# Two gather tiles instead of three, a reordered last step, and interleaved rows in a spiking recommender kernel on one Trainium2 core

## The chip, the cores and the metric

The kernel runs on one core of a Trainium2 chip. A core has five engines that run their own instruction streams and meet through semaphores: TensorE (PE; its weight loads are shown apart as PEld), VectorE (DVE), ScalarE (ACT), GpSimd (POOL) and SyncE (SP), and 16 DMA engines that all of them share. The metric is the device time of one execution in microseconds (us); the median of three runs stands for the kernel.

## The reference

1024 users have 50 items each, out of a table of 100001 rows of 128 numbers. Row 0 of the table counts as zero. All arithmetic is float32.

```python
emb = emb_table.at[0].set(0.0)
e = emb[seq]                              # (1024, 50, 128)
prefix = jnp.cumsum(e, axis=1)
t_idx = jnp.arange(1, T + 1)
denom = jnp.minimum(t_idx[None, :], lengths[:, None])
uF = prefix / denom[:, :, None]
mean = uF.mean(axis=0); var = uF.var(axis=0)      # over the users, for each step and column
y = (uF - mean) * lax.rsqrt(var + BN_EPS) * gamma + beta
# for each of the 50 steps, with x the step's y and v starting at 0:
#   v = v + (x - v) / 2;  spike = v >= 1;  v = v - spike
uF_out = spikes.mean(axis=0)              # (1024, 128)
scores = uF_out @ emb.T                   # (1024, 100001)
```

The output is 1024 x 100001 float32, 409.6 MB, and writing it is most of the traffic.

## The kernel before

The work is written in program order under a manual schedule: each engine runs its instructions in the order in which the code emits them, and a tile pool of `bufs=n` makes the writer of a tile wait until the tile n places earlier has been read.

**Opening (lines 174 to 252).** SP loads the indices (`idx`, line 175, users n*128 + p on partition p, column block n), the lengths, row 0 of the table, gamma and beta, and then 38 blocks of 1024 table rows that the second stage needs (`fetch`). `isz` and `rb` are two tiles of 1024 columns that are transposed on TensorE: one marks the indices that are 0, the other holds 1/length. They take two of the three tiles of the pool `gather`.

**The 50 steps (lines 296 to 370).** The users lie on the free axis, the 128 columns of the table on the partitions. For step t:

- `gather(t + 2)` at the head of the step issues eight indirect DMAs on GpSimd (line 195), each of which fetches 128 table rows of 512 B into a column block of the tile `e`. Step t reads its own tile `e`, gathered two steps ahead. Only the first of the eight waits for the tile to be free.
- TensorE adds the transposed rows to the running sums in the two PSUM banks `pre[0]` and `pre[1]` (line 308, eight transposes); `correct` (line 268) adds in advance a term that takes row 0 of the table out again. `correct(t + 1)` overwrites nothing, but it must follow Vector's reading of `pre` in step t, so the transposes of step t + 1 come after the last uF of step t.
- Vector makes uF, half by half (`uF`, line 317; `bs`, line 318), and from it mean and variance (`mv`, line 322). ScalarE takes the root (line 326) and subtracts the mean (line 327).
- Vector completes the scale `a` (lines 333 to 338). Meanwhile it finishes the previous step: `rest` (line 284) makes `negv` = spike - v from `d`, which ScalarE made as v - 1 (`over`, line 280), and `spiked` (line 287) adds the spikes to `count`.
- ScalarE applies scale and shift (line 342), Vector adds -0.5 * negv (`step`, line 345): the new v.

In steps 42 and 44 two blocks of the table are transposed and split ahead of time (`prepare`: TensorE, ScalarE and Vector).

In the last step, `rest` and `spiked` of step 48 come first, ahead of the first uF. Behind the loop the last v is made in three groups of columns, 128, 512 and 384, each with its own tile of counts (`countA`, `countB`, `countC`): ScalarE computes x for all three, Vector does `step` and `spiked` for A, then both for B and C. TensorE warms up on 16 dummy transposes (line 377) meanwhile. A block of 128 users is then one 128-column piece of these counts, n = 0 to 7, the first being `countA`.

**The scores (lines 395 to 491).** For chunks of 2, 3 or 6 blocks of 1024 table rows, and for each of the eight blocks of users, TensorE multiplies the counts with a high and a low part of the table block (line 153), Vector and ScalarE take turns in scaling the result out of PSUM (lines 469 and 471), and SP stores up to 24 KB for each of 128 output rows (`store`, line 162): rows n*128 to n*128 + 127. ScalarE issues the loads of the remaining table blocks. New blocks are transposed and split between the products.

Of the kernel before, what the change touches and what calls it, by code (L numbers as in the profile page):

```python
# [12 lines left out]
F32 = mybir.dt.float32  # L13
# [4 lines left out]
AF = mybir.ActivationFunctionType  # L18
ALU = mybir.AluOpType

P = 128
BN_EPS = 1e-5
# [3 lines left out]
BANK = 512  # L26
# [10 lines left out]
def rec_kernel(  # L37
# [9 lines left out]
    nc = tc.nc  # L47
    B, T = seq.shape
    N, D = table.shape
    NB = B // P  # L50
    assert D == P and B == HALF and T <= P // 2


# [9 lines left out]
    countA = const.tile([P, P], F32R, tag="countA", name="countA")  # L63
    countB = const.tile([P, BANK], F32R, tag="countB", name="countB")
    countC = const.tile([P, B - BANK - P], F32R, tag="countC", name="countC")
# [93 lines left out]
            )  # L159

    def store(n, c0, o):
        nc.sync.dma_start(out=out[n * P : (n + 1) * P, c0 : c0 + o.shape[1]], in_=o)


    with ExitStack() as ph:
        once = ph.enter_context(tc.tile_pool(name="once", bufs=1))
        lp = ph.enter_context(tc.tile_pool(name="lif", bufs=1))
        sp = ph.enter_context(tc.tile_pool(name="stats", bufs=3))
        up = ph.enter_context(tc.tile_pool(name="uF", bufs=2))
        gp = ph.enter_context(tc.tile_pool(name="gather", bufs=3))  # L170
        accp = ph.enter_context(tc.tile_pool(name="acc", bufs=1, space=bass.MemoryType.PSUM))
        vp = ph.enter_context(tc.tile_pool(name="v", bufs=1, space=bass.MemoryType.PSUM))

        idx = once.tile([P, NB, T], I32, tag="idx", name="idx")
        nc.sync.dma_start(out=idx, in_=seq.rearrange("(n p) t -> p n t", p=P))
        len_i = once.tile([P, NB], I32, tag="len_i", name="len_i")
        nc.sync.dma_start(out=len_i, in_=lengths.rearrange("(n p) -> p n", p=P))
        r0 = once.tile([P, D], F32, tag="r0", name="r0")
        nc.sync.dma_start(out=r0, in_=table[0:1, :].to_broadcast([P, D]))
        gb = once.tile([P, 2], F32, tag="gb", name="gb")  # L180
        nc.sync.dma_start(out=gb[:, 0:1], in_=gamma.rearrange("(d o) -> d o", o=1))
        nc.sync.dma_start(out=gb[:, 1:2], in_=beta.rearrange("(d o) -> d o", o=1))
        first = group(0)
# [8 lines left out]
        def gather(t):  # L192
            es[t] = gp.tile([P, B], F32, tag="e", name=f"e_{t}")
            for n in range(NB):
                nc.gpsimd.indirect_dma_start(  # L195
                    out=es[t][:, n * P : (n + 1) * P],
                    out_offset=None,
                    in_=table,
                    in_offset=bass.IndirectOffsetOnAxis(ap=idx[:, n, t : t + 1].bitcast(U32), axis=0),
                )  # L200

        make_identity(nc, ident)
        isz = gp.tile([P, NB, P], F32, tag="e", name="isz")
        rb = gp.tile([P, NB, P], F32, tag="e", name="rb")
        gather(0)

        nc.vector.memset(isz, 0.0)
# [2 lines left out]
        zps = vp.tile([P, B], F32, tag="v1", name="zps")  # L210
        for n in range(NB):
            nc.tensor.transpose(zps[:, n * P : (n + 1) * P], isz[:, n, :], ident)
        zT = once.tile([P, B], F32R, tag="zT", name="zT")
        nc.scalar.copy(zT, zps)
        r0hi = once.tile([P, D], F32R, tag="r0hi", name="r0hi")
        nc.scalar.copy(r0hi, r0)
        r0n = once.tile([P, D], F32, tag="r0n", name="r0n")
# [14 lines left out]
        rlen = once.tile([P, B], F32, tag="rlen", name="rlen")  # L232
        nc.vector.tensor_copy(rlen, rps)

        hgb = once.tile([P, 2], F32, tag="hgb", name="hgb")
        nc.vector.tensor_scalar_mul(hgb[:, 0:1], gb[:, 0:1], 0.25)
        nc.vector.tensor_scalar_mul(hgb[:, 1:2], gb[:, 1:2], 0.5)
        eps = once.tile([P, 1], F32, tag="eps", name="eps")
        nc.vector.memset(eps, BN_EPS)
# [2 lines left out]
        count = once.tile([P, B], BF16, tag="count", name="count")  # L242
        nc.vector.memset(count, 0.0)

        negv = once.tile([P, B], F32, tag="negv", name="negv")
# [3 lines left out]
        pre = [accp.tile([P, BANK], F32, tag=f"pre{h}", name=f"pre{h}") for h in range(B // BANK)]  # L249
# [33 lines left out]
        def rest(d, v):  # L283
            nc.vector.scalar_tensor_tensor(negv, d, 0.0, v, ALU.is_ge, ALU.subtract)  # L284

        def spiked(out, cs, v):
            nc.vector.scalar_tensor_tensor(out, v, V_TH, count[:, cs], ALU.is_ge, ALU.add)  # L287

        whole = slice(0, B)
        halves = [slice(h * BANK, (h + 1) * BANK) for h in range(B // BANK)]  # L290
        v = None
# [3 lines left out]
        gather(1)  # L295
        for t in range(T):
            last = t == T - 1
            if t + 2 < T:
                gather(t + 2)
            e = es.pop(t)  # L300
            if last:
                rest(d, v)
                spiked(count, whole, v)
            uF = up.tile([P, B], F32, tag="uF", name=f"uF_{t}")
            bs = sp.tile([P, B // BANK, 6], F32, tag="bs", name=f"bs_{t}")
            for h, cs in enumerate(halves):
                for k in range(0, BANK, P):
                    nc.tensor.matmul(  # L308
                        pre[h][:, k : k + P],
                        lhsT=e[:, h * BANK + k : h * BANK + k + P],  # L310
                        rhs=ident,
                        start=False,
                        stop=last,
                        is_transpose=True,
                        skip_group_check=True,
                    )
                nc.vector.scalar_tensor_tensor(uF[:, cs], rlen[:, cs], 1.0 / (t + 1), pre[h], ALU.max, ALU.mult)  # L317
                nc.vector.bn_stats(bs[:, h, :], uF[:, cs])  # L318
            if not last:
                correct(t + 1, l)  # L320
            mv = sp.tile([P, 2], F32, tag="mv", name=f"mv_{t}")
            nc.vector.bn_aggr(mv, bs.rearrange("p h s -> p (h s)"))  # L322


            r = sp.tile([P, 1], F32, tag="r", name=f"r_{t}")
            nc.scalar.activation(r, mv[:, 1:2], AF.Sqrt, bias=eps)  # L326
            nc.scalar.activation(uF, uF, AF.Identity, bias=mv[:, 0:1], scale=-1.0)


            if t and not last:  # L330
                rest(d, v)

            nc.vector.reciprocal(r, r)
            q = sp.tile([P, 1], F32, tag="q", name=f"q_{t}")
            nc.vector.scalar_tensor_tensor(q, mv[:, 1:2], BN_EPS, r, ALU.add, ALU.mult)
            nc.vector.tensor_scalar(q, q, r, 3.0, ALU.mult, ALU.subtract)
            a = sp.tile([P, 1], F32, tag="a", name=f"a_{t}")
            nc.vector.tensor_scalar(a, q, r, hgb[:, 0:1], ALU.mult, ALU.mult)  # L338


            def x(vt, cs):
                nc.scalar.activation(vt, uF[:, cs], AF.Identity, bias=hgb[:, 1:2], scale=a)  # L342

            def step(vt, cs):
                nc.vector.scalar_tensor_tensor(vt, negv[:, cs], -0.5, vt, ALU.mult, ALU.add)  # L345

            if not last:
                vt = vp.tile([P, B], F32, tag=f"v{t % 2}", name=f"v_{t}")
                x(vt, whole)
                if t:  # L350
                    spiked(count, whole, v)
                step(vt, whole)
                v = vt
                d = over(t, v)
                if t + 2 < T:
                    l = only(t + 2)

                if t in (T - 8, T - 6):
                    q = (t - T + 8) // 2
                    pair(q)  # L360
                    prepare(q, vp.tile([P, HALF], F32, tag="v1", name=f"pt_{q}"))
                    if q == TWICE - 1:
                        for k in range(TWICE):
                            rows[GROUP + k] = first[:, k, :]
                        nc.sync.dma_start(
                            out=first[:, :TWICE, :],
                            in_=table[GROUP * HALF : (GROUP + TWICE) * HALF, :].rearrange(
                                "(q p k) d -> p q (k d)", p=P, k=KQ
                            ),
                        )  # L370
# [5 lines left out]
        for k in range(2 * KQ):  # L376
            nc.tensor.transpose(warm[:, k % KQ * P : (k % KQ + 1) * P], ident, ident)
        vC = vp.tile([P, B - BANK - P], F32, tag="v1", name="vC")
        groups = [
            (slice(0, P), pre[0][:, :P], countA),  # L380
            (slice(P, P + BANK), pre[1], countB),
            (slice(P + BANK, B), vC, countC),
        ]
        for cs, vt, _ in groups:
            x(vt, cs)
        cs, vt, first = groups[0]
        step(vt, cs)
        spiked(first, cs, vt)
        for cs, vt, _ in groups[1:]:
            step(vt, cs)  # L390
        for cs, vt, c in groups[1:]:
            spiked(c, cs, vt)


# [2 lines left out]
        for q, (pool, tag, po) in enumerate(((gp, "e", po0), (up, "uF", po1))):  # L397
            o = pool.tile([P, HALF], F32, tag=tag, name=f"o_0_{q}")
# [26 lines left out]
    for c, W in enumerate(WIDTHS):  # L425
# [30 lines left out]
        for n in range(NB):  # L456
            if c == 0 and n == 0:
                continue
            pool, tag, most = turns[blocks % len(turns)]
            blocks += 1  # L460
            o = pool.tile([P, most * HALF], F32, tag=tag, name=f"o_{c}_{n}")
# [16 lines left out]
            if c or n > 1:  # L478
                store(n, q0 * HALF, o[:, : min(N, q1 * HALF) - q0 * HALF])
# [3 lines left out]
            if n in (1, 4) and c >= MIDDLE and to_fetch < parts:  # L483
                g, k = divmod(to_fetch - TWICE, GROUP)
                if k or to_split >= (g - 1) * GROUP + TWICE:
                    if k == 0:
                        r = group(g)
# [23 lines left out]
```

## Time and profile before

| | us |
|---|---|
| median of three runs | 1648.53 (1646.59 to 1648.60) |
| the profiled execution: its time | 1649.66 |
| the profiled execution: its span | 1647.8 |
| first gather issued | 3.96 |
| last gather issued | 565.6 |
| first store issued | 586.71 |
| busy: PE, DVE, ACT, POOL | 1069.7, 944.0, 669.2, 381.4 |

The span is cut in two stages by the first store. Ahead of it DMA engines move some 47 GB/s once the opening loads are done (about 60 us), and the granted TensorE clock is 0.50; behind it they move 416 GB/s. A line of the timeline gives start, duration, engine, source line, operation and tiles, and in brackets how long the engine sat idle before it and what ended that. "issue" is idle time for which the profile shows no cause, "remote" is an end that it puts down to no engine or queue of this core. In the table of stretches each row gives, for a piece of the span, busy time and number of instructions of PE, PEld, DVE, ACT and POOL, the granted clock, the DMA engines' busy share and what they moved. In the list of waits the figures are the total, the number and the longest. The starts of matmuls are recorded, their ends are modelled.

### The profile page before, as it was taken

What the parts mean: (1) busy time and instruction counts of PE and PEld (TensorE: products, weight loads), DVE (VectorE), ACT (ScalarE), POOL (GpSimd) and SP (SyncE); (2) the same over time, 40 slices, a digit from 0 to 9 for tenths busy, and PEclk for the clock granted to TensorE, in tenths of its full rate; (3) what the DMA queues carried; (4) which work ended last, traced back from release to release, by engine and by line L of the source; (5) the groups of instructions that cost most, each with busy time, mean ns of one, the idle gap of its engine ahead of it and who ended that gap; (6) DMA issues with size and microseconds to landing.
All of it is one profiled execution on the core that took longest, in us unless ns stands there. A gap on an engine that the chain in (4) does not pass through costs nothing.

```text
span 1647.8 us, 12231 instructions
## 1 busy us (share of the span) xinstructions
PE 1069.7 (65%) x4450; PEld 816.8 (50%) x4450; DVE 944.0 (57%) x1122; ACT 669.2 (41%) x697; POOL 381.4 (23%) x406
## 2 busy tenths in 40 slices
PE   4233332222322488888988888888887888888884
PEld 2022221111211376666866666666666666666763
DVE  5366665656665866556755455555555555555552
ACT  2133332323322455455644444444444444444442
POOL 7676666666666500000000000000000000000000
PEclk7555555555555589999999999989999999999998
DMA  9511111111111269999999999999999999999998
GB/s 345 209 50 46 46 47 46 45 46 49 46 45 46 64 285 416 405 421 418 399 425 429 430 429 423 416 434 418 427 427 416 416 421 417 428 427 423 396 431 342
DMA packets 53689, 488.12 MB, mean 296 GB/s; under 512 B 11995, under 2 KB 12796, under 8 KB 32380
## 3 DMA queue, kind: packets, MB, share of 16 engines
q1 hardware_dynamic: 32256, 429.81, 62.0%
q0 software_dynamic: 12800, 26.24, 5.9%
q10 hardware_dynamic: 8572, 31.28, 4.8%
q8 instruction: 35, 0.57, 0.1%
q14 instruction: 26, 0.21, 0.0%
HBM read 77.69 MB, written 409.60 MB: 296 GB/s over the span
## 4 chain that ended last, share of the span: by engine, by line
DMA 45%; DVE 20%; PE 11%; another core or an unknown queue 10%; ACT 7%; issue 4%; POOL 1%; ACTq 0%; SPq 0%; DVEq 0%
DMA scores<-o 45%; PE po L153 10%; ACT o L471 5%; DVE bs L318 4%; DVE uF L317 3%; DVE v L345 3%; DVE negv L284 3%; DVE count L287 2%; ACT v L342 2%; DVE o L469 1%; POOL e L195 1%; PE pre L268 1%; DVE a L338 1%; DVE mv L322 1%
## 5 line engine op out<-in xcount | busy, mean ns | idle before, releaser
L469 DVE TENSOR_SCALAR o<-po 128x1024 f32<-128x1024 f32 x391 | 464.4, 1221 | 344.7 <-DMA scores<-o 310.4
L471 ACT ACTIVATE o<-po 128x1024 f32<-128x1024 f32 (+1 forms) x391 | 389.7, 1018 | 538.8 <-DMA scores<-o 324.6
L195 POOL DMA_INDIRECT e<-in_L_rec_emb_table,idx x400 | 380.7, 952 | 184.6 <-issue 114.9
L153 PE MATMUL po<-pairs,countB 128*128 128x512 f32 x1136 | 305.1, 414 | 59.8 <-ACT o L471 42.8
L268 PE MATMUL pre<-zT,ls 128*128 128x512 f32 x100 | 78.7, 789 | 364.1 <-DVE uF L317 267.1
L153 PEld LDWEIGHTS po<-pairs,countB 128*128 128x128 f32 x1136 | 218.0, 197 | 122.9 <-ACT o L471 57.9
L153 PE MATMUL po<-pairs,countC 128*128 128x512 f32 x852 | 236.4, 424 | 44.8 <-ACT o L471 44.8
L268 PEld LDWEIGHTS pre<-zT,ls 128*128 128x128 f32 x100 | 28.8, 289 | 407.7 <-DVE uF L317 297.2
L153 PEld LDWEIGHTS po<-pairs,countC 128*128 128x128 f32 x852 | 167.0, 203 | 90.7 <-ACT o L471 56.3
L317 DVE SCALAR_TENSOR_TENSOR uF<-rlen,pre 128x512 f32<-128x512 f32 x100 | 68.0, 680 | 168.1 <-remote 101.2
L146 DVE TENSOR_TENSOR pairs<-pt,pairs 128x1024 fp32r<-128x1024 f32 x71 | 86.3, 1222 | 93.3 <-ACT pairs L145 93.2
L326 ACT ACTIVATE r<-mv,eps 128x1 f32<-128x1 f32 x50 | 14.7, 295 | 283.2 <-DVE mv L322 179.5
L123 PE MATMUL pt<-ident,rows 128*128 128x128 f32 x782 | 113.8, 294 | 8.7 <-issue 4.9
L123 PEld LDWEIGHTS pt<-ident,rows 128*128 128x128 f32 x782 | 103.5, 155 | 27.5 <-issue 13.2
L308 PE MATMUL pre<-ident,e 128*128 128x128 f32 x400 | 101.0, 422 | 16.1 <-DMA e<-in_L_rec_emb_table,idx 14.9
L153 PE MATMUL po<-hi,countB 128*128 128x512 f32 x216 | 89.1, 412 | 19.4 <-ACT o L471 16.8
L308 PEld LDWEIGHTS pre<-ident,e 128*128 128x128 f32 x400 | 83.6, 221 | 31.6 <-DMA e<-in_L_rec_emb_table,idx 21.8
L153 PE MATMUL po<-lo,countB 128*128 128x512 f32 x216 | 86.7, 403 | 0.0
L280 ACT ACTIVATE d<-v,less 128x1024 bf16<-128x1024 f32 x49 | 54.5, 1113 | 63.6 <-DVE v L345 45.4
L153 PE MATMUL po<-hi,countC 128*128 128x512 f32 (+1 forms) x162 | 68.4, 422 | 15.7 <-ACT o L471 15.7
L145 ACT CAST pairs<-pt 128x1024 fp32r<-128x1024 f32 x71 | 71.8, 1012 | 15.4 <-PE pt L123 15.2
L153 PE MATMUL po<-pairs,countA 128*128 128x512 f32 x284 | 71.3, 394 | 8.2 <-ACT o L471 8.1
(67 smaller groups left out, 844.5 us busy)
## 6 DMA issues: line engine op xcount, KB each, us to landing
scores<-o SPq DMA_DIRECT2D x96, 3072.0 KB
scores<-o SPq DMA_DIRECT2D x32, 1536.0 KB
scores<-o SPq DMA_DIRECT2D x30, 1024.0 KB
rows<-in_L_rec_emb_table ACTq DMA_DIRECT2D x19, 1536.0 KB
scores<-o SPq DMA_DIRECT2D x8, 2896.5 KB
rows<-in_L_rec_emb_table SPq DMA_DIRECT2D x6, 3072.0 KB
e<-in_L_rec_emb_table,idx POOLq DMA_INDIRECT x400
rows<-in_L_rec_emb_table SPq DMA_DIRECT2D x1, 1024.0 KB
```

The costliest lines, as they stand in the source:

```text
L123: nc.tensor.transpose(pt[:, k0 : k0 + kw], r[:kw, k0 : k0 + D], ident[:kw, :kw])
L145: nc.scalar.copy(vh, vp)
L146: nc.vector.tensor_tensor(vl, vp, vh.bitcast(F32), ALU.subtract)
L153: nc.tensor.matmul(po[:, :kw], lhsT=counts[n], rhs=part[:, k0 : k0 + kw], start=j == 0, stop=j == 1,)
L195: nc.gpsimd.indirect_dma_start(out=es[t][:, n * P : (n + 1) * P], out_offset=None, in_=table, in_offset=bass.IndirectOffsetOnAxis(ap=idx[: ...
L268: nc.tensor.matmul(pre[h], lhsT=l, rhs=zT[:, h * BANK : (h + 1) * BANK], start=t == 0, stop=False, skip_group_check=True,)
L280: nc.scalar.activation(d, v, AF.Identity, bias=less)
L308: nc.tensor.matmul(pre[h][:, k : k + P], lhsT=e[:, h * BANK + k : h * BANK + k + P], rhs=ident, start=False, stop=last, is_transpose=True, ...
L317: nc.vector.scalar_tensor_tensor(uF[:, cs], rlen[:, cs], 1.0 / (t + 1), pre[h], ALU.max, ALU.mult)
L318: nc.vector.bn_stats(bs[:, h, :], uF[:, cs])
L469: nc.vector.tensor_scalar_mul(o[:, h0 : h0 + hw], po[:, :hw], 1.0 / T)
L471: nc.scalar.mul(o[:, h0 : h0 + hw], po[:, :hw], 1.0 / T)
```

## The change

The change has four parts.

1. The pool `gather` has two tiles instead of three. `isz` and `rb` take the two tiles of the pool `uF` instead. `gather(t + 2)` is issued behind the transposes of step t, whose tile it overwrites, instead of at the head of the step.
2. In the last step the comparison and the addition to `count` for step 48 are two GpSimd instructions of 1024 columns (`s`, in the room of `zT`), and `rest` stands between the two halves of uF. The order on Vector is: uF and bs of the first half, `rest`, `near`, uF and bs of the second half.
3. The first 128 columns of the last step run on Vector alone: `near` = -0.5 * negv + beta/2, `centred` = (uF - mean) * (-gamma/4), `q` in another grouping of the same factors, `vA` = centred * q + near, then `countA`. `a` is computed behind that for the other two groups. ScalarE subtracts the mean for groups B and C behind the loop. On Vector, `step` and `spiked` follow each other within a group.
4. Partition p holds users 8p to 8p + 7 instead of p, 128 + p, ...: the loads of indices and lengths are contiguous for each partition, and a store of block n writes the output rows 8p + n.

```diff
--- before.py
+++ after.py
@@ -48,6 +48,7 @@
     B, T = seq.shape
     N, D = table.shape
     NB = B // P
+    outs = out.rearrange("(p n) c -> n p c", n=NB)
     assert D == P and B == HALF and T <= P // 2
 
 
@@ -159,7 +160,7 @@
             )
 
     def store(n, c0, o):
-        nc.sync.dma_start(out=out[n * P : (n + 1) * P, c0 : c0 + o.shape[1]], in_=o)
+        nc.sync.dma_start(out=outs[n, :, c0 : c0 + o.shape[1]], in_=o)
 
 
     with ExitStack() as ph:
@@ -167,14 +168,14 @@
         lp = ph.enter_context(tc.tile_pool(name="lif", bufs=1))
         sp = ph.enter_context(tc.tile_pool(name="stats", bufs=3))
         up = ph.enter_context(tc.tile_pool(name="uF", bufs=2))
-        gp = ph.enter_context(tc.tile_pool(name="gather", bufs=3))
+        gp = ph.enter_context(tc.tile_pool(name="gather", bufs=2))
         accp = ph.enter_context(tc.tile_pool(name="acc", bufs=1, space=bass.MemoryType.PSUM))
         vp = ph.enter_context(tc.tile_pool(name="v", bufs=1, space=bass.MemoryType.PSUM))
 
         idx = once.tile([P, NB, T], I32, tag="idx", name="idx")
-        nc.sync.dma_start(out=idx, in_=seq.rearrange("(n p) t -> p n t", p=P))
+        nc.sync.dma_start(out=idx, in_=seq.rearrange("(p n) t -> p n t", n=NB))
         len_i = once.tile([P, NB], I32, tag="len_i", name="len_i")
-        nc.sync.dma_start(out=len_i, in_=lengths.rearrange("(n p) -> p n", p=P))
+        nc.sync.dma_start(out=len_i, in_=lengths.rearrange("(p n) -> p n", n=NB))
         r0 = once.tile([P, D], F32, tag="r0", name="r0")
         nc.sync.dma_start(out=r0, in_=table[0:1, :].to_broadcast([P, D]))
         gb = once.tile([P, 2], F32, tag="gb", name="gb")
@@ -200,8 +201,8 @@
                 )
 
         make_identity(nc, ident)
-        isz = gp.tile([P, NB, P], F32, tag="e", name="isz")
-        rb = gp.tile([P, NB, P], F32, tag="e", name="rb")
+        isz = up.tile([P, NB, P], F32, tag="uF", name="isz")
+        rb = up.tile([P, NB, P], F32, tag="uF", name="rb")
         gather(0)
 
         nc.vector.memset(isz, 0.0)
@@ -232,8 +233,9 @@
         rlen = once.tile([P, B], F32, tag="rlen", name="rlen")
         nc.vector.tensor_copy(rlen, rps)
 
-        hgb = once.tile([P, 2], F32, tag="hgb", name="hgb")
+        hgb = once.tile([P, 3], F32, tag="hgb", name="hgb")
         nc.vector.tensor_scalar_mul(hgb[:, 0:1], gb[:, 0:1], 0.25)
+        nc.vector.tensor_scalar_mul(hgb[:, 2:3], gb[:, 0:1], -0.25)
         nc.vector.tensor_scalar_mul(hgb[:, 1:2], gb[:, 1:2], 0.5)
         eps = once.tile([P, 1], F32, tag="eps", name="eps")
         nc.vector.memset(eps, BN_EPS)
@@ -295,12 +297,11 @@
         gather(1)
         for t in range(T):
             last = t == T - 1
-            if t + 2 < T:
-                gather(t + 2)
             e = es.pop(t)
             if last:
-                rest(d, v)
-                spiked(count, whole, v)
+                s = once.tile([P, B], F32, tag="zT", name="s")
+                nc.gpsimd.tensor_single_scalar(s, d, 0.0, ALU.is_ge)
+                nc.gpsimd.tensor_tensor(count, count, s, ALU.add)
             uF = up.tile([P, B], F32, tag="uF", name=f"uF_{t}")
             bs = sp.tile([P, B // BANK, 6], F32, tag="bs", name=f"bs_{t}")
             for h, cs in enumerate(halves):
@@ -316,6 +317,12 @@
                     )
                 nc.vector.scalar_tensor_tensor(uF[:, cs], rlen[:, cs], 1.0 / (t + 1), pre[h], ALU.max, ALU.mult)
                 nc.vector.bn_stats(bs[:, h, :], uF[:, cs])
+                if last and h == 0:
+                    rest(d, v)
+                    near = once.tile([P, P], F32, tag="r0", name="near")
+                    nc.vector.tensor_scalar(near, negv[:, :P], -0.5, hgb[:, 1:2], ALU.mult, ALU.add)
+            if t + 2 < T:
+                gather(t + 2)
             if not last:
                 correct(t + 1, l)
             mv = sp.tile([P, 2], F32, tag="mv", name=f"mv_{t}")
@@ -324,7 +331,13 @@
 
             r = sp.tile([P, 1], F32, tag="r", name=f"r_{t}")
             nc.scalar.activation(r, mv[:, 1:2], AF.Sqrt, bias=eps)
-            nc.scalar.activation(uF, uF, AF.Identity, bias=mv[:, 0:1], scale=-1.0)
+            if last:
+                centred = once.tile([P, P], F32, tag="r0hi", name="centred")
+                nc.vector.tensor_scalar(centred, uF[:, :P], mv[:, 0:1], hgb[:, 2:3], ALU.subtract, ALU.mult)
+                w = sp.tile([P, 1], F32, tag="w", name="w")
+                nc.vector.tensor_scalar_add(w, mv[:, 1:2], BN_EPS)
+            else:
+                nc.scalar.activation(uF, uF, AF.Identity, bias=mv[:, 0:1], scale=-1.0)
 
 
             if t and not last:
@@ -332,10 +345,18 @@
 
             nc.vector.reciprocal(r, r)
             q = sp.tile([P, 1], F32, tag="q", name=f"q_{t}")
-            nc.vector.scalar_tensor_tensor(q, mv[:, 1:2], BN_EPS, r, ALU.add, ALU.mult)
-            nc.vector.tensor_scalar(q, q, r, 3.0, ALU.mult, ALU.subtract)
             a = sp.tile([P, 1], F32, tag="a", name=f"a_{t}")
-            nc.vector.tensor_scalar(a, q, r, hgb[:, 0:1], ALU.mult, ALU.mult)
+            if last:
+                nc.vector.tensor_scalar(q, w, r, r, ALU.mult, ALU.mult)
+                nc.vector.scalar_tensor_tensor(q, q, 3.0, r, ALU.subtract, ALU.mult)
+                vA = once.tile([P, P], F32, tag="r0n", name="vA")
+                nc.vector.scalar_tensor_tensor(vA, centred, q, near, ALU.mult, ALU.add)
+                spiked(countA, slice(0, P), vA)
+                nc.vector.tensor_mul(a, q, hgb[:, 0:1])
+            else:
+                nc.vector.scalar_tensor_tensor(q, mv[:, 1:2], BN_EPS, r, ALU.add, ALU.mult)
+                nc.vector.tensor_scalar(q, q, r, 3.0, ALU.mult, ALU.subtract)
+                nc.vector.tensor_scalar(a, q, r, hgb[:, 0:1], ALU.mult, ALU.mult)
 
 
             def x(vt, cs):
@@ -376,19 +397,12 @@
         for k in range(2 * KQ):
             nc.tensor.transpose(warm[:, k % KQ * P : (k % KQ + 1) * P], ident, ident)
         vC = vp.tile([P, B - BANK - P], F32, tag="v1", name="vC")
-        groups = [
-            (slice(0, P), pre[0][:, :P], countA),
-            (slice(P, P + BANK), pre[1], countB),
-            (slice(P + BANK, B), vC, countC),
-        ]
+        groups = [(slice(P, P + BANK), pre[1], countB), (slice(P + BANK, B), vC, countC)]
         for cs, vt, _ in groups:
+            nc.scalar.activation(uF[:, cs], uF[:, cs], AF.Identity, bias=mv[:, 0:1], scale=-1.0)
             x(vt, cs)
-        cs, vt, first = groups[0]
-        step(vt, cs)
-        spiked(first, cs, vt)
-        for cs, vt, _ in groups[1:]:
+        for cs, vt, c in groups:
             step(vt, cs)
-        for cs, vt, c in groups[1:]:
             spiked(c, cs, vt)
```

## The prediction

> **What bounds the kernel now.** I read the page's slices first: the span is two stages. In the first 14 slices GpSimd is busy and the DMA engines lie at a tenth or two; from slice 15 on the DMA engines are full.
>
> ```profile
> POOL 7676666666666500000000000000000000000000
> PEclk7555555555555589999999999989999999999998
> DMA  9511111111111269999999999999999999999998
> ```
>
> The stage of stores (first store at 586.7, end 1647.8, 1061.1 us) moves 416 GB/s with a DMA share of 0.99; no engine there is the bound, so it takes what its bytes take. The change reaches the time by when that stage begins and by how the stores are laid out. So I went to the 50 steps, first to GpSimd's waits and then to busy time by stretches cut where GpSimd starts again after a wait (columns: PE, PEld, DVE, ACT, POOL busy and count, clock, DMA share, GB/s).
>
> ```profile
> POOL e L195 <- issue: 114.9, 377, 0.3
> POOL e L195 <- remote: 55.5, 10, 7.8
> ```
>
> ```profile
> 264.00:309.10 45.10, 13.18 (x40) 8.82 (x40) 28.88 (x50) 14.62 (x16) 30.38 (x32) 0.50 0.18 47
> ...
> 354.30:398.80 44.50, 13.18 (x40) 8.83 (x40) 28.68 (x50) 14.62 (x16) 30.45 (x33) 0.50 0.19 48
> 398.80:433.50 34.70, 9.39 (x30) 6.62 (x30) 21.28 (x37) 10.96 (x12) 22.81 (x24) 0.50 0.18 46
> ```
>
> 400 gathers at 0.94 us busy and 0.30 of issue are 1.25 each, 500 us; ten long waits add 55. In the steady stretches the pattern repeats every 32 gathers (four steps): 40 us of issuing, 5.3 of waiting, 45.1. What GpSimd waits for shows in the timeline of one such stretch.
>
> ```profile
> 288.49 1.91 PE L308 MATMUL pre<-ident,e 128*128 128x128 f32 x8
> ...
> 303.95 0.69 DVE L317 SCALAR_TENSOR_TENSOR uF<-rlen,pre 128x512 f32<-128x512 f32 x1 [9.68 <-issue]
> ...
> 308.89 0.69 DVE L317 SCALAR_TENSOR_TENSOR uF<-rlen,pre 128x512 f32<-128x512 f32 x1 [3.53 <-remote]
> ...
> 309.13 0.94 POOL L195 DMA_INDIRECT e<-in_L_rec_emb_table,idx  x1 [5.30 <-remote]
> ```
>
> The transposes of step 24 are recorded within 2 us at 288.5, yet the two L317 that wait for them run at 303.95 and 308.89. TensorE's semaphore steps in the trace come at 290.6, 293.4, 296.2, 298.3, 301.1, 306.7: one per 2 to 3 us instead of per 0.2. So TensorE really crawls there, while GpSimd issues on until it needs the tile of step 24 (last issue 302.88, its data moved by 305.1). TensorE is quick again only some 4 us after the gather traffic has stopped. I don't know the cause. I read it as something that fills with gather traffic and drains at a fixed rate: after each stop some 24 us pass until TensorE slows, and cycles of 32 and of 24 gathers give nearly one rate (45.1/32 = 1.41, 34.7/24 = 1.446 us a gather). Vector's own chain needs only 7.35 us a step (v at 321.20 and 328.55), GpSimd 10.0.
>
> The last bound is the tail, from v of step 48 to the first product:
>
> ```profile
> 576.98 1.22 DVE L284 SCALAR_TENSOR_TENSOR negv<-d,v 128x1024 f32<-128x1024 bf16 x1 [1.18 <-ACT d L280]
> 578.12 1.22 DVE L287 SCALAR_TENSOR_TENSOR count<-v,count 128x1024 bf16<-128x1024 f32 x1
> 579.25 0.68 DVE L317 SCALAR_TENSOR_TENSOR uF<-rlen,pre 128x512 f32<-128x512 f32 x1
> ...
> 583.22 0.27 DVE L338 TENSOR_SCALAR a<-q,r,hgb 128x1 f32<-128x1 f32 x1
> 584.11 0.29 DVE L345 SCALAR_TENSOR_TENSOR pre<-negv,pre 128x128 f32<-128x128 f32 x1 [0.61 <-ACT pre L342]
> 584.44 0.29 DVE L287 SCALAR_TENSOR_TENSOR countA<-pre,count 128x128 fp32r<-128x128 f32 x1
> ```
>
> Here Vector is the path: 1.18 of waiting for d, then negv and count, before the last uF, whose transposes had ended at 572.9.
>
> **What the Trainium skill says.** *GPSIMD Engine Reference*, § Elementwise — side-by-side cycle accounting: an fp32 add of two tensors of 2048 columns takes 4497 ns on GpSimd; the trace before has no arithmetic there to compare. *SBUF — State Buffer*, § SBUF: two separate sides: GpSimd and a Vector operation in a two-port mode, or with two SBUF inputs, exclude each other for a whole instruction; not visible before, since GpSimd only gathers (a gather took 1.16 and 2.26 us once each, the rest 0.94). *DMA: Bandwidth & Descriptors*, § Latency and other measured facts: HBM rows whose pitch is a large power of two copy at half rate or less, and a few KiB of padding restore it. § Specifications of the same page: pieces under 512 B are below line rate; the idx load here is of 200 B pieces, 1024 of them, and took 2.94 us.
>
> **The change part by part.**
> *Start.* idx becomes 128 runs of 1600 B. GpSimd's first gather waits for it (starts at 3.96). A load of that size still has its fixed latency: a gather lands 2.3 us after its start, so I take 2.2 us instead of 2.94, -0.7; bounds -1.2 and 0. isz and rb move to the uF pool: gathers of step 1 lose a wait that cost nothing (they follow at 1.25), and uF of steps 0 and 1 wait for transposes that were over at 6.5 and 12. Nothing.
>
> *Two tiles.* A gather of step t+2 now waits for the transposes of step t, not t-1, and all later gathers queue behind it on GpSimd; nothing else is in that queue until the last step, SP's isn't passed. In clear running the wait is free: gathers of step t take 10.0 us, land 2.3 after, transposes take 1.9, so tile t is free 4 to 5 us after its last issue, while GpSimd is busy 10 us with t+1. In a slow patch I count from a restart R. With two tiles only one landed tile is waiting, the steps run just behind the gathers, and the transposes of R's third tile end at R+21.4. TensorE slows at R+24; GpSimd still issues the fourth and fifth tile until R+40, then stops, as it does now (302.88 + 0.94 is R+39.8 from 264.0). So a cycle stays 32 gathers in 45 us: 0. The cover is 24 - 21.4 = 2.6 us; the rival below prices its loss. A gain is left at the end: now the steps lag the gathers (last gather lands at 567.9, transposes end at 572.9, v of step 48 ends at 575.8, made later by the two `prepare` calls); just behind them, transposes would end near 568.5 and v near 567.3, up to 8.5 us sooner. Where the last slow patch falls decides how much of that comes; it can also fall on the last tile, about +5. I take -3.
>
> *Last step.* uF of the first half starts at v's end, 575.8. In order: uF and bs 1.4, negv 1.22 (d was ready at 576.9), near some 0.25 (128 columns; r0n, the same shape, took 0.23), second half 1.4: aggregate at 580.0 instead of 582.0. After the reciprocal: two q of 0.2, then vA and countA at 0.33 each, without a, the two ACT calls and their 0.61 of waiting: the first product at 582.0 instead of 584.85, -2.85. centred and w lie under ACT's square root (0.36 of idle now). countB and countC: centring moves behind on ACT (0.65 and 0.5), but TensorE has eight products (2.6 us) of countA before it needs countB, which comes 2.3 after countA: hidden; without cover 0.5. GpSimd's count: compare and add of 1024 columns, by the page's figure an estimated 1 + 2.3 us from 577.0, ready near 580.4, needed at 581.6; hidden if so, and at double price 2 us late. Near and centred may have to wait for GpSimd's add by the exclusion above, up to 2 us. So -2.85 to 0; I take -1.5.
>
> *Stores.* Row pitch within a store goes from 400,004 B to 3,200,032 B: 3 MiB and 53 KiB, far from an aliasing multiple by the page's figures. Packets, bytes and order stay. I take 0; bounds -5 and +20 (2% of 1061).
>
> Sum: -0.7 - 3 - 1.5 = -5.2 on the profiled execution: span 1647.8 to 1642.6, its time 1649.66 (1.86 around the span) to 1644.5. The median of the runs, 1648.53, lies 1.1 below that execution, so 1643.3, given as 1643.5.
>
> **The rivals.** *Two tiles lose gathers (slower).* Place: the wait of the first gather of tile t+2. If TensorE slows before the third tile's transposes are through, that is before R+21.4, GpSimd stops at R+30 and each cycle is 24 gathers. The trace prices it: 1.446 against 1.41 us, 0.037 x 360 gathers = +13 us, less 2.2 for start and tail: 1659.5. For it: the onset varies from 21 to 32 us. Against: one steady drain rate, which would cancel most of it. *Nothing but the ends.* Cycles and lag stay, the port lock eats part of the tail: -1 to -3, 1646.5. *The stores' layout costs 1%*: +10.6 - 5.2, 1654. All 416 GB/s are near what this stage ever shows (up to 442 in 2 us), so it could hardly gain.
>
> **How the numbers follow.** Forecast 0.45 (1636 to 1646), two tiles losing 0.27 (1652 to 1668), ends only 0.20 (1644.5 to 1648), stores 0.08. A measurement of this kernel tells about 0.2%, 3.3 us, from no change. Faster (under 1645.2): most of the forecast and a little of the ends, 0.42; same: the rest of both, 0.24; slower: 0.34. The range 1636 to 1662 leaves out one in ten on each side; the forecast's own is 1636 to 1646.
>
> **What would show it.** Right: gather stretches still at 1.40 to 1.42 us a gather, ten long waits of GpSimd near 5 us, last L317 of step 49 nearer to the last gather than 13.6 us, first store 5 us earlier, 416 GB/s. Wrong: cycles of 24 gathers or waits over 8 us; near or centred starting when GpSimd's add ends; a store rate under 412 GB/s. If the stage of steps loses its long waits altogether, my reading of the slow patches is wrong, and the gain is far larger.

## The result and the profile after

| | before | after |
|---|---|---|
| median, six runs each | 1648.51 us | 1638.54 us |
| ratio, 95% interval | | 0.9933 (0.9918 to 0.9949) |
| span of the profiled execution | 1647.8 | 1636.5 |
| first gather issued | 3.96 | 3.53 |
| last gather issued | 565.63 | 561.97 |
| end of v of step 48 | 575.80 | 563.79 |
| first product | 584.88 | 573.64 |
| first store | 586.71 | 576.25 |
| first store to the end | 1061.1 | 1060.3 |

The time falls by 10.0 us, forecast were 5.2. Between the two profiled executions the span falls by 11.3 us. By the table, 0.4 us of these come from the start, 3.2 from the gathers between the first and the last, 8.4 from the shorter way from the last gather to the end of v of step 48 (10.17 to 1.82), and 0.8 from the stores; from the end of v to the first store 1.5 us are lost (10.91 to 12.46).

The slices look as before but for the granted TensorE clock, which is high in the first stage too (an experiment below takes that up):

```profile
POOL 7666676666766600000000000000000000000000
PEclk9999999999997599999999998999999999899998
DMA  9511111111112189999999999999999999999998
```

GpSimd's long waits add up to nearly as much as before. Before they came to 64.0 us, the 55.5 put down to "remote" and 8.5 more put down to TensorE's `correct`:

```profile
POOL e L195 <- PE pre L268: 8.5, 2, 5.4
```

After they come to 59.7: 42.6 and 12.4 of the same two kinds, and one of 4.7 listed under "issue". Two stretches from restart to restart are shown below the waits; they hold 32 gathers in 45 us, as before (other stretches hold 8 to 40).

```profile
POOL e L196 <- issue: 115.9, 366, 4.7
POOL e L196 <- remote: 42.6, 11, 5.9
POOL e L196 <- PE pre L270: 12.4, 3, 6.1
```

```profile
306.70:352.00 45.30, 16.25 (x41) 8.78 (x41) 30.05 (x51) 14.62 (x16) 30.43 (x32) 1.00 0.18 46
352.00:397.00 45.00, 16.22 (x40) 8.31 (x40) 27.97 (x48) 14.62 (x16) 30.44 (x32) 1.00 0.18 47
```

The timeline of the last step:

```profile
562.56 1.23 DVE L366 SCALAR_TENSOR_TENSOR v<-negv,v 128x1024 f32<-128x1024 f32 x1 [0.20 <-issue]
...
565.03 2.78 POOL L303 TENSOR_SCALAR s<-d 128x1024 f32<-128x1024 bf16 x1 [2.11 <-ACT d L282]
566.84 0.69 DVE L318 SCALAR_TENSOR_TENSOR uF<-rlen,pre 128x512 f32<-128x512 f32 x1 [3.05 <-remote]
...
567.89 2.14 POOL L304 TENSOR_TENSOR count<-count,s 128x1024 bf16<-128x1024 bf16 x1
568.17 1.20 DVE L286 SCALAR_TENSOR_TENSOR negv<-d,v 128x1024 f32<-128x1024 bf16 x1
569.41 0.70 DVE L323 TENSOR_SCALAR near<-negv,hgb 128x128 f32<-128x128 f32 x1
570.03 0.68 DVE L318 SCALAR_TENSOR_TENSOR uF<-rlen,pre 128x512 f32<-128x512 f32 x1
...
573.20 0.29 DVE L289 SCALAR_TENSOR_TENSOR countA<-vA,count 128x128 fp32r<-128x128 f32 x1
```

uF, which the change lets start at the end of v (563.79), starts 3.05 us later, put down to "remote": TensorE was crawling over the last tile. That wait stands where before the wait for d, negv and count stood. near takes 0.70 us.

### The profile page after: what moved, and what is told of

Its sections match the earlier page's. It is cut to its first block, busy times and chain, and to the rows that moved or that the text cites. A ratio compares the mean times of both kernels' runs of the same rounds, so it can differ in the third digit from the quotient of the medians.

```text
span 1636.5 us, 12239 instructions
## 1 busy us (share of the span) xinstructions
PE 1090.1 (67%) x4450; PEld 809.3 (49%) x4450; DVE 942.9 (58%) x1125; ACT 668.0 (41%) x697; POOL 388.3 (24%) x408
## 4 chain that ended last, share of the span: by engine, by line
DMA 47%; PE 12%; DVE 11%; POOL 10%; another core or an unknown queue 7%; issue 6%; ACT 6%; ACTq 0%; SPq 0%; DVEq 0%; POOLq 0%
DMA scores<-o 44%; PE po L154 11%; POOL e L196 10%; ACT o L485 4%; DVE bs L319 2%; DVE uF L318 2%; DMA rows<-in_L_rec_emb_table 2%; DVE v L366 2%; DVE negv L286 1%; DMA e<-in_L_rec_emb_table,idx 1%; DVE o L483 1%; DVE count L289 1%; ACT v L363 1%; PE pt L124 1%
## 5 line engine op out<-in xcount | busy, mean ns | idle before, releaser
L309 PE MATMUL pre<-ident,e 128*128 128x128 f32 x400 | 129.3, 438 | 90.6 <-DMA e<-in_L_rec_emb_table,idx 70.7
L309 PEld LDWEIGHTS pre<-ident,e 128*128 128x128 f32 x400 | 79.9, 207 | 141.5 <-DMA e<-in_L_rec_emb_table,idx 107.7
L154 PE MATMUL po<-hi,countB 128*128 128x512 f32 x216 | 88.7, 411 | 18.6 <-ACT o L485 13.1
```

The costliest lines, as they stand in the source:

```text
L154: nc.tensor.matmul(po[:, :kw], lhsT=counts[n], rhs=part[:, k0 : k0 + kw], start=j == 0, stop=j == 1,)
L309: nc.tensor.matmul(pre[h][:, k : k + P], lhsT=e[:, h * BANK + k : h * BANK + k + P], rhs=ident, start=False, stop=last, is_transpose=True, ...
```

## Experiments

Theory A: what piles up with gather traffic and slows TensorE drains at a fixed rate, so the gathers end when they did; two tiles gain because the steps follow right behind the gathers. B: the gain is the start and the new last step. C: it is TensorE's clock (mean 0.791 before, 0.943 after). Kernels that stand under one heading below ran on one chip, a different one for each of the three headings, with runs of before between them.

**Parts undone or alone** (before: 1651.41 us there).

```diff
 three_tiles = after, but
-gp = tile_pool(name="gather", bufs=2)      # isz, rb in up, gather(t + 2) behind the transposes
+gp = tile_pool(name="gather", bufs=3)      # isz, rb in gp, gather(t + 2) at the head of the step
 two_tiles_alone = before, with the reverse of these lines
 old_rows = after, but
-seq.rearrange("(p n) t -> p n t", n=NB)    # and lengths, and out
+seq.rearrange("(n p) t -> p n t", p=P)
 old_last_step = before, with bufs=2 and the rows of after
```

> The kernel after the change with its first part undone: three gather tiles, gather(t + 2) at the head of the step. Theory A (two tiles make the steps follow right behind the gathers, and the lag at the end goes): the gain goes, 1646 to 1648, last uF again 10 us or more behind the last gather. Rival B (the gain is the start and the new last step): stays at 1638 to 1640. Rival C (the gain is TensorE's higher granted clock, 0.943 against 0.791): the time follows the clock, whichever that is in this run.

Measured 1650.52 us, ratio 0.9993 (0.9981 to 1.0004): the gain is gone.

> The kernel before the change with two gather tiles and the later gather, nothing else. Theory A: nearly the whole gain, 1638 to 1641, last uF some 5 us behind the last gather. Rival B: 1647 to 1649. Rival C: follows the granted clock.

Measured 1645.88 us, ratio 0.9957 (0.9943 to 0.9970): 7.1 us by the ratio, between A and B, nearer to A.

> The kernel after the change with partition p holding rows p, 128 + p and so on again. Theory A: first gather 0.4 us later, stores at the same 416 GB/s, 1639. A rival that puts gain or loss into the layout of the stores expects 1634 or less, or 1643 or more.

Measured 1644.34 us, ratio 0.9959 (0.9947 to 0.9971); the stores took 1061.0 us.

> The kernel after the change with the last step as before (count on VectorE, rest ahead of the first uF, scale a, three groups). Theory A: the new last step took 9.85 us from the end of v of step 48 to the first product, the old one 9.08, so no loss: 1637 to 1639. Rival B: 2.85 us of the gain are lost, 1641.5.

Measured 1645.20 us, ratio 0.9960 (0.9945 to 0.9975).

The tiles carry most of the change. B falls with three_tiles, which has the new start and last step and no gain. C falls too: that run has a clock of 0.939 and the time of before. Two expectations missed: by the ratio, old_rows and old_last_step lie some 6.7 us under before, where A expected about 10. The time of old_rows lies where the rival of the stores' layout stood, and 6.7 us is about the gain that B left to old_last_step. The traces speak against both readings: the stores of old_rows took 1061.0 us, as with the new rows, and in old_last_step the way from the end of v to the first store took 10.90 us, less than the 12.46 of the change. The whole change didn't run on this chip, so its 0.9933 stands beside these ratios from another chip, and what rows and last step add beside two tiles can't be told from the times: each kernel with two tiles and less than the whole change lies at 0.996, and two_tiles_alone ran from 1641.5 to 1652.5.

The traces say where the spread comes from. For each profiled execution (one for each row; before_again and the two no_pool_count kernels ran on the third chip, below), us per gather from the first to the last, us from the last gather's issue to the end of v of step 48, and from the first store to the end:

| kernel | a gather | v behind the gathers | stores |
|---|---|---|---|
| before | 1.408 | 10.2 | 1061.1 |
| before_again | 1.403 | 9.8 | 1060.5 |
| three_tiles | 1.409 | 13.6 | 1061.8 |
| after | 1.400 | 1.8 | 1060.3 |
| old_rows | 1.408 | 3.4 | 1061.0 |
| old_last_step | 1.407 | 5.0 | 1060.4 |
| no_pool_count | 1.399 | 1.3 | 1060.3 |
| two_tiles_alone | 1.406 | 13.1 | 1061.6 |
| no_pool_count_centre_first | 1.398 | 11.7 | 1060.5 |

Gathers and stores go at one rate in all nine, with two tiles or three. Only the middle column moves. With three tiles it is 10 to 14 us; with two it is 1 to 5, but 12 to 13 where a slow patch fell on the last tiles. These two executions are the slowest of their kernels (1652.45 and 1645.09 us).

**The change once more, and pacing, on a second chip** (before: 1577.18 us there).

> The kernel after the change once more, beside the others on one chip: 0.993 of before. Gathers at 1.40 to 1.41 us each whatever the number of tiles, stores 1060 to 1062 us; the lag from the last gather to the last step's uF is what moves between executions.

Measured 1579.46 us, ratio 1.0014 (1.0007 to 1.0021). Neither the gain nor the level was expected. In this trace GpSimd has no long wait at all:

```profile
POOL e L196 <- issue: 113.0, 371, 0.3
POOL e L196 <- DMA e<-in_L_rec_emb_table,idx: 7.3, 24, 0.3
POOL e L196 <- DMA idx<-in_r_seq: 2.2, 1, 2.2
```

The gathers go at 1.26 us, their issue rate, and the stores take 1060.1 us as ever: the 59 us to the first time of this kernel lie ahead of the first store (516.71 us against 576.25), where the slow patches were. Another difference goes with that: the trace holds 9688 records of DMA landings, against 4417 in the first trace of the same kernel and 4262 to 4565 in the others with patches. What is missing are the records of the gathers: 6396 of the 9688 belong to them, but only 1219 of the 4417, while of the other DMAs 3292 and 3198 are there. The patches occur where records were lost; that doesn't say which of the two brings the other.

```diff
 pace_128, pace_320 = after, with
     nc.gpsimd.indirect_dma_start(...)
+    nc.gpsimd.memset(idle, 0.0)            # idle: 128 or 320 columns
```

> After the change, with a GpSimd memset of 128 columns behind each gather, some 0.15 to 0.2 us more per gather. If something drains at a fixed rate of one gather in 1.41 us, gathers at 1.40 to 1.45 us leave nothing to pile up: TensorE's slow patches and GpSimd's long waits go, the gathers end within -5 to +20 us of before, 1635 to 1658. If the patches come by time (each 45 us) or with TensorE's own work, they stay, and 60 to 80 us are added: 1700 or more.

Measured 1620.84 us, ratio 1.0275 (1.0261 to 1.0289).

> The same with 320 columns, some 0.35 us more per gather: 1.6 us each. Drain at a fixed rate: no long waits at all, gathers end near 640, 1710 to 1720. Patches by time or by TensorE's work: waits stay, 1760 or more.

Measured 1681.28 us, one run.

Neither time is among those expected, which started from a level some 60 us higher. Both only show what a slower gather costs where nothing piles up (1.363 and 1.516 us each): they don't tell the theories apart.

> After the change with four gathers a step instead of eight; the second half of the users reuses the rows of the first, so the output is another one. TensorE, VectorE and ScalarE do the same work as before. Drain of gather traffic: four gathers in 7.35 us are 1.84 us each, under the rate, so no slow patches, steps at 7.4 us, last uF near 390, time near 1460. If TensorE's own instructions fill what drains, patches come as often per step as before, 5 to 18 us each four steps: 1500 or more.

```diff
-for n in range(NB):
+for n in range(NB // 2):                   # in gather; lhsT=e[:, k : k + P] for both halves
```

Measured 1465.02 us, one run: the time that A names, but without patches around it, so it is no evidence for A.

**Pacing on a third chip, where the patches occur** (before: 1647.68 us there).

> The kernel before once more, for its trace beside those of this call. Where semaphore records are complete (some 9700 landings against 4300) there are no slow patches: gathers at 1.249 us without long waits, last gather near 504, first product near 512, time near 1577. Where they are lost, ten long waits as in its first trace, near 1650.

Measured 1646.86 us, with 4262 landing records and fourteen waits of GpSimd put down to "remote" (55.3 us).

> The paced kernel again. With slow patches in this call's traces: a spacing of 1.347 is under the 1.41 at which they let gathers through, so fewer and shorter waits, gathers still ending near 565, time within 5 us of the kernel after the change; patches by time or by TensorE's work: 40 us more. Without slow patches: 1621 again.

Measured 1641.22 us, ratio 0.9965 (0.9955 to 0.9976). GpSimd's waits in the paced kernel, for gathers and for the added memset:

```profile
POOL e L197 <- issue: 68.9, 388, 1.5
POOL e L197 <- remote: 13.6, 8, 3.3
POOL idle L203 <- remote: 7.0, 8, 1.5
```

The spacing within a run of gathers is 1.347 us instead of 1.249, 39 us over 400. The waits shrink by nearly that, from 55.3 to 20.6, and the whole goes at 1.415 us a gather.

Patches that come by time are ruled out by the traces. In the kernel before, Vector's waits for the crawling transposes begin every 45 us (at 113, 157, 203, 248, 294 and 338 us). In the paced kernel they come irregularly, and in two stretches, steps 20 to 23 and 30 to 33, there are none: the second uF starts 3.1 us after the last gather of its tile, as on the chip without patches (3.0). In before it starts 13.6 us or more behind that gather in every step from 3 on. Yet the rate is the same, and so it is with two tiles or three. So one rate bounds the stage.

What it is that drains at this rate, pacing can't tell, since a step holds eight gathers and the same work of the other engines whatever the spacing. TensorE's own instructions are unlikely: behind the first store of the kernel before it ran 207 matmuls in 50 us, in the steps 40 in 45 us.

```profile
600.00:650.00 50.00, 45.06 (x207) 34.05 (x206) 29.75 (x25) 25.09 (x25) 0.00 (x0) 1.00 1.01 417
```

That the lost records are those of the gathers makes the gathers the likelier cause. A kernel with fewer gathers a step didn't run on a chip with patches, so it is not shown.

```diff
 no_pool_count = after, but
-    s = once.tile(...)
-    nc.gpsimd.tensor_single_scalar(s, d, 0.0, ALU.is_ge)
-    nc.gpsimd.tensor_tensor(count, count, s, ALU.add)
     nc.vector.tensor_scalar(near, ...)
+    spiked(count, whole, v)
 no_pool_count_centre_first = that, and ahead of the last step's x
+for cs, vt, _ in groups:                   # a loop of its own for x
```

> After the change, with the count of step 48 on VectorE behind near, nothing but gathers on GpSimd. Theory D (GpSimd's arithmetic costs twice: it holds near and centred up, 0.3 and 1.1 us, and each gather takes 952 instead of 944 ns, 400 x 8 ns = 3.1 us): without slow patches 4 us less than the kernel after the change, 1575 beside 1577 of before. With slow patches the gathers' rate stays 1.41 and only about 1 us is gained. Rival E (the 8 ns and the held-up instructions come from the two tiles or the rows): no gain, since VectorE takes 1.22 us more.

Measured 1639.29 us, ratio 0.9947 (0.9929 to 0.9966), not to be told from the change's 0.9933 on another chip. The time doesn't decide between D and E, the trace does. Here is near without arithmetic on GpSimd, and then in the kernel old_rows, beside GpSimd's add:

```profile
L319 DVE TENSOR_SCALAR near<-negv,hgb x1: 287/287/287, 569.3 to 569.3; 128x128 f32<-128x128 f32 x1
```

```profile
L322 DVE TENSOR_SCALAR near<-negv,hgb x1: 2097/2097/2097, 573.3 to 573.3; 128x128 f32<-128x128 f32 x1
```

A gather takes 944 ns here and 952 in the change (medians). Both have two tiles and the new rows, so E's cause for the 8 ns and the held-up instructions falls.

> The same, and ScalarE subtracts the mean for groups B and C ahead of both x, in its wait for a (2.0 us in the trace). The first store comes 0.6 us earlier than in the kernel with the count moved alone, the time is 0.6 us less; if the first store is not what sets the end, the same.

Measured 1640.12 us, ratio 0.9950 (0.9931 to 0.9969). First product to first store is 1.97 us against 2.70 in no_pool_count: the 0.6 us are there in the trace, and lost in the spread of the time. Neither version is shown to beat the change.

## Why the prediction was right

The term that names the mechanism, the lag behind the last gather, brought most of the gain. In the two profiled executions the terms came as -0.4 (start), -3.2 (gathers), -8.4 (lag), +1.5 (last step) and -0.8 (stores), where -0.7, 0, -3, -1.5 and 0 were forecast. That the kernel met a chip with slow patches was luck: the prediction gave no chance to one without them.

**The start** was put at -0.7 and gave -0.43: the first gather's wait for idx fell from 2.65 to 2.23 us. Right in kind.

**The gathers' rate** was to stay at 1.40 to 1.42 us: 1.400. The step that named a fixed rate holds, and the paced kernel showed it; that gather traffic is what fills was a reading, and stays one. A change of 0.6% within the forecast range was still worth 3.2 us. The ten waits that the prediction counted (55.5 us) were twelve, with the two put down to `correct` (64.0). The cycle that I counted out (transposes through at R+21.4, GpSimd stopped at R+40) was too neat: in the profile after, GpSimd's long waits come after 8 to 40 gathers. The rate didn't depend on it; as I read it, an earlier stop only lets the rest drain earlier. For the same reason the rival of two tiles losing gathers (+13 us) didn't come.

**The lag at the end** is the term that was mis-sized. The prediction bounded it at -8.5 and +5 and took -3; v of step 48 ended 8.4 us nearer to the last gather. Halving was fair for one execution (two of the six traces with two tiles in the table show the lag undiminished), but the likeliest case was most of the gain. The 13.6 us in the prediction's list of signs are those of the first of the two uF in step 49; it started 4.9 us behind the last gather after the change.

**The last step** was put at -1.5, within -2.85 and 0, and the profile shows +1.5 from the end of v to the first store. In this execution a slow patch held the first uF up by 3.05 us, which undid the saved wait. Two executions without that wait, three_tiles and the paced kernel on the third chip, show the step by itself: from the end of v 7.88 us to the first product and 10.59 to the first store, against 9.08 and 10.9 in the four executions with the old step. So it gained 1.2 and 0.3 us, not 2.85 and 1.5.

Two terms of that sum were mis-sized. GpSimd's compare took 2.78 us, where I had reckoned 1 (the add took 2.14; the 2.3 estimated from the Trainium skill's page *GPSIMD Engine Reference*, § Elementwise — side-by-side cycle accounting, agrees). So its add fell on near or centred, and these waited for it: near took 0.70 us here and 2.10 in old_rows, against 0.29 without arithmetic there; centred took 1.96 us in three_tiles and 1.62 in the paced kernel, against 0.35. Those 1.6 us (1.3 in the paced kernel) are most of what is missing to the first product. The exclusion in *SBUF — State Buffer*, § SBUF: two separate sides, is thus visible, and with it a sign that the prediction had named for being wrong, near or centred held by GpSimd's add. Without slow patches it struck centred too:

```profile
510.30 2.15 POOL L304 TENSOR_TENSOR count<-count,s 128x1024 bf16<-128x1024 bf16 x1
...
511.21 1.32 DVE L336 TENSOR_SCALAR centred<-uF,mv,hgb 128x128 f32<-128x128 f32 x1
512.45 0.14 DVE L338 TENSOR_SCALAR w<-mv 128x1 f32<-128x1 f32 x1
```

centred ends when GpSimd's add does. The second term is ScalarE's later centring, which I called hidden: it delays the first store by some 0.7 us (2.70 against 1.97 in the last two kernels above).

**The stores**: 0 forecast, 1060.3 against 1061.1 us measured, and 1060.1 to 1061.8 in all twelve other traces, with either row order. The row pitch of 3,200,032 B costs nothing that these show.

**Where it doesn't hold.** The forecast is one for executions with slow patches, though it doesn't say so. Without them the same change is 0.14% slower. The prediction also expected a far larger gain if the long waits went; on the second chip the level of before fell as well (1577.18 us), and there was no gain. A plausible sum for the loss is 3.1 us for gathers that take 8 ns more, against 0.4 from the start; before wasn't profiled there, so that is argued and not shown. Also open: what piles up (the lost records point to the recording, which no experiment here switched off), and whether rows and last step, worth 0.4 and 0.3 us by the traces, show in the time at all.

## What to carry to other kernels

When an engine's instructions are recorded as quick and its readers still wait, look at when its semaphore steps really come, and pace the suspected traffic: if the total stays, a rate is the bound, and depth of buffering only decides how far the consumers lag at the end. Compare a gain on more than one chip before it is called a property of the kernel. Before work moves to GpSimd, look for VectorE operations on its path that run at the same time: a 0.3 us instruction on VectorE can last until GpSimd's ends, here up to 2.1 us.

## What the runs showed of the hardware

- TensorE's transposes, recorded 0.2 us apart, completed one per 2 to 3 us in stretches of the first stage (288 to 307 us of before). Such patches are in the ten traces in which records of gather landings are missing, and in none of the four in which they are complete. The same kernel took 1638.5 us with them and 1579.5 without.
- With arithmetic on GpSimd in the program an indirect gather took 952 to 961 ns instead of 944 (medians of eight traces against six).
- A compare of 1024 columns on GpSimd (bf16 to f32) took 2.78 us, longer than the add of two tensors behind it, 2.14.
- In each of the eight traces with that add, the small VectorE operation that met it (near or centred, 128 columns, 0.29 and 0.35 us alone) ended within 0.1 us of the add's end. Under the compare alone near took 0.29 us in three_tiles and 0.52 in after_again.
- Doubling the granted TensorE clock in the first stage (0.50 to 1.00 by the stretches) left its rate as it was; the kernel before itself ran at a mean of 0.791 and of 0.942, with 1.408 and 1.403 us a gather.
